# A graph layer on one core: rows of B picked in float32 by partition halves, with counts, copies and node layers rearranged

## The chip, the cores and the metric

The kernel runs on one core of a Trainium2 chip. The time is device microseconds of that core, the median of several runs. A profile is one further execution, recorded by the hardware profiler; its span and its durations are its own.

## What is computed

A message-passing layer on 12,500 nodes with 64 features and 212,500 edges, sorted by `dst`:

```python
h = jnp.maximum(_layernorm(x, axis=-1), 0.0)
edge_in = jnp.concatenate([h[row], h[col], dist], axis=1)      # row = src, col = dst
e = jax.nn.silu(edge_in @ eW1 + eb1)
e = jax.nn.silu(e @ eW2 + eb2)
agg = jax.ops.segment_sum(e, row, num_segments=h.shape[0])
node_in = jnp.concatenate([h, agg], axis=1)
out = x + jax.nn.silu(node_in @ nW1 + nb1) @ nW2 + nb2
```

Everything is float32. The sum goes by `src`, in which the edges are not sorted.

## The kernel before

The first edge product is split: A = h @ eW1[:64] + eb1 and B = h @ eW1[64:128], one row of each for every node, so that an edge needs A[src] + B[dst] + dist * eW1[128]. Both tables lie in HBM (`ta`, `tb`), each row as three bf16 parts that add up to the float32 value.

**Prologue.** `x` is loaded, normalised by five groups of 20 columns, transposed on TensorE, and multiplied to B by `product(1, ...)` (lines 169 to 192), 25 times, four columns each. Edge lists are loaded as 104 rows of 2048; `rowsS` and `auxS` hold, for each edge, its place in a window of B, its bucket, and three bf16 parts of the weight; they go to HBM as `rows` and `aux`.

**Blocks of 1024 edges.** There are 208, in 11 chunks. Since edges are sorted by `dst`, a block needs at most 112 consecutive rows of B, its window `win`. `load` (372) issues on SP the broadcast of the block's places and buckets to 112 partitions (`bc`), the window (384) and the weight's parts (386). `count` (389) runs on VectorE: `pick` (395) is a one-hot matrix of 112 window rows by 1024 edges, `oh` (397) a one-hot of 100 buckets by edges, `run` a running count along the edges (400, a scan that takes its start from `end`, 406), and 408 keeps each edge's own count. `send` (417): TensorE turns the counts into ranks (427) and picks the rows of B plus weight by three bf16 matmuls a tile of 128 edges over 115 rows (435); ScalarE copies them to `qs` (442), VectorE copies the place of the source node beside them (449), and GpSimd scatters 128 rows per indirect DMA to the bucket's free slots in the HBM tensor `q` (454). 1661 such scatters are issued.

**Steps of 512 slots.** 525 steps read `q` back bucket by bucket. `fetch` (489) loads `qt` and `a3` through SP, five batches ahead. Per step, on TensorE: `lr` (521) spreads the places, `pt` transposes the rows (535) and adds the rows of A by a one-hot (542), `p` is the second product (573), `seg` the sum (587). VectorE makes the two one-hots (526, 553) and adds to `aggT` (598); ScalarE computes the two activations (546, 577) and writes the bias (567). `feeds` computes A by `product(0, ...)` beside the first blocks.

**Nodes.** In the last chunk every batch of four node columns ends in `nodes` (333): two `z` products (341 over all 128 partitions, 342 over 64), an activation, and `o` (346 bias, 348 product), then `xr` is added (351).

**Order.** TensorE, VectorE, ScalarE and SP run in the order in which the program is written, by `turn` (605): per step a list of stages of different steps, with four gaps in which a piece of a block, of a feed or of the nodes is put. GpSimd has its own queue. Four PSUM buffers `mm` are shared in turn by `lr`, `pt`, `qp`, `ab`, `z` and `o`. `win` has four fixed buffers, `bc` and `pick` four, `qs` eight.

Of the kernel before, what the change touches and what calls it, by code (L numbers as in the profile page):

```python
# [28 lines left out]
F32 = mybir.dt.float32  # L29
F16 = mybir.dt.float16  # L30
# [10 lines left out]
WL = 112  # L41
BLK = 1024
TB = BLK // P
# [14 lines left out]
def tile_gnn(ctx: ExitStack, tc: tile.TileContext, x, src, dst, ew, eW1, eb1, eW2, eb2, nW1, nb1, nW2, nb2, out):  # L58
# [39 lines left out]
    def rows16(dma, to, of):  # L98

        for part in (slice(0, WL), slice(WL, L)):  # L100
            dma(to[part], of[part])
# [10 lines left out]
    eb1r = const.tile([1, 2, H], F32, name="eb1r")  # L112
    for t in range(2):
        nc.gpsimd.dma_start(eb1r[:, t, :], rows_of(eb1, 1))
# [14 lines left out]
    nb2r = const.tile([1, G, D], F32, name="nb2r")  # L129
    for t in range(G):  # L130
        nc.gpsimd.dma_start(nb2r[:, t, :], rows_of(nb2, 1))
# [14 lines left out]
    nc.vector.tensor_copy(nodes1, nodes_i)  # L146
    ones = const.tile([1, P], F32, name="ones")
# [15 lines left out]
    tb = dram.tile([P * NB, 3 * H], BF16, name="tb")  # L163
    rows = dram.tile([NP, 2, 2, BLK], BF16, name="rows")
    aux = dram.tile([NP, 2, 3, BLK], BF16, name="aux")
# [3 lines left out]
    def product(s, b0, hr, ps, tag, sb, sb2, queue):  # L169

        parts = sb2.tile([P, G, 3, H], BF16, name="parts")
        by = parts.rearrange("l (i a) s h -> l a i s h", a=2)
        rest = sb.tile([P, 2, G // 2, H], F32, name="prest", tag="e1")
        abs_ = []
        for a in range(2):

            half = slice(a * D, (a + 1) * D)
            ab = ps.tile([P, G // 2, H], F32, name="ab", tag=tag)
            if s == 0:
                nc.tensor.matmul(ab, ones, eb1r, start=True, stop=False)  # L180
            for i in range(G // 2):
                nc.tensor.matmul(ab[:, i], hr[half, i, :], w1[half, s, :], start=s == 1, stop=s == 1 or i == G // 2 - 1)
            nc.scalar.copy(by[:, a, :, 0, :], ab)
            abs_.append(ab)
        yield
        for a in range(2):
            nc.vector.tensor_tensor(rest[:, a], abs_[a], by[:, a, :, 0, :], op=OP.subtract)  # L187
        nc.scalar.copy(by[:, :, :, 1, :], rest)
        yield
        nc.vector.tensor_tensor(by[:, :, :, 2, :], rest, by[:, :, :, 1, :], op=OP.subtract)  # L190
        yield
        queue.dma_start(tables[s][:, b0 : b0 + G, :], parts.rearrange("p b s f -> p b (s f)"))
# [4 lines left out]
    base_i = const.tile([1, 2, NP], I32, name="base_i")  # L197
    NW = 4
    wins = [const.tile([P, 3, H], BF16, name=f"win{i}") for i in range(NW)]

    with tc.tile_pool(name="pro", bufs=1) as pro, tc.tile_pool(name="norm", bufs=2) as np_, tc.tile_pool(
# [12 lines left out]
        ewR = pro.tile([NP, PAIR], F32, name="ewR")  # L214
        pad_i = pro.tile([1, PAD], I32, name="pad_i")
        nc.gpsimd.memset(pad_i, N)
        pad_f = pro.tile([1, PAD], F32, name="pad_f", tag="pad_i")
        nc.gpsimd.memset(pad_f, 0.0)
        vec = lambda v, lo, n, m: bass.AP(tensor=v.tensor, offset=v.offset + lo, ap=[[m, n], [1, m]])
        for to, v, pad in (  # L220
            (dstR, dst, vec(dst, E - PAD, 1, PAD)),
            (srcR, src, pad_i),
            (ewR, ew, pad_f),
        ):
            for p0, p1 in ((0, NP // 16 * 16), (NP // 16 * 16, NP - 1)):
                nc.scalar.dma_start(to[p0:p1, :], vec(v, p0 * PAIR, p1 - p0, PAIR))
            nc.scalar.dma_start(to[NP - 1 : NP, :LAST], vec(v, (NP - 1) * PAIR, 1, LAST))
            nc.scalar.dma_start(to[NP - 1 : NP, LAST:], pad)
# [36 lines left out]
        fv = f.rearrange("p (g e) -> p g e", g=2)  # L265
        lo = pro.tile([NP, 2], F32, name="lo")
        nc.vector.tensor_reduce(lo, fv, AX.X, OP.min)
        nc.vector.tensor_scalar(lo, lo, float(N - WL), None, op0=OP.min)
        hi = pro.tile([NP, 2], F32, name="hi")
        nc.vector.tensor_reduce(hi, fv, AX.X, OP.max)  # L270
        lot = nps.tile([1, 2, NP], F32, name="lot", tag="tr")
        for g in range(2):
            nc.tensor.transpose(lot[:, g, :], lo[:, g : g + 1], ident[:NP, :NP])
# [4 lines left out]
        nc.vector.tensor_tensor(  # L278
            rowsS[:, :, 0, :], fv, lo[:, :, None].to_broadcast([NP, 2, BLK]), op=OP.subtract
        )  # L280
# [15 lines left out]
        auxS = pro.tile([NP, 2, 3, BLK], BF16, name="auxS")  # L296
        ev = ewR.rearrange("p (g e) -> p g e", g=2)
        parts3(pro, auxS[:, :, 0, :], auxS[:, :, 1, :], auxS[:, :, 2, :], ev, [NP, 2, BLK], tag="t")
        nc.sync.dma_start(aux, auxS)


# [13 lines left out]

        d3 = pro.tile([P, 3, H], BF16, name="d3")
        parts3(pro, d3[:, 0, :], d3[:, 1, :], d3[:, 2, :], w1d, [P, H])
        for win in wins:
            nc.sync.dma_start(win[WL : WL + 3, :, :], d3[:3, :, :])

# [4 lines left out]
    def nodes_in(B, sb):  # L325
        b = B * G
        xr = sb.tile([L, G, D], F32, name="xr")
        rows16(nc.sync.dma_start, xr, x_rows[:, b : b + G, :])
        hr = sb.tile([P, G // 2, P], F32, name="hrn")
        nc.sync.dma_start(hr, hd[:, b // 2 : b // 2 + G // 2, :])  # L330
        return xr, hr

    def nodes(B, xr, hr, ps, sb, tag):
# [3 lines left out]
        zs = sb.tile([P, 2, G // 2, L], F32, name="zs")  # L337
        for a in range(2):
            half = slice(a * D, (a + 1) * D)
            z = ps.tile([P, G // 2, L], F32, name="z", tag=tag)  # L340
            nc.tensor.matmul(z, w1g, aggT[:, b + a : b + G : 2, :], start=True, stop=False)  # L341
            nc.tensor.matmul(z, w1n[half, :], hr[half, :, :L], start=False, stop=True)  # L342
            nc.scalar.activation(zs[:, a], z, AF.Silu, bias=nb1c)
        yield
        o = ps.tile([L, G, D], F32, name="o", tag=tag)
        nc.tensor.matmul(o, ones[:, :L], nb2r, start=True, stop=False)  # L346
        for t in range(G):
            nc.tensor.matmul(o[:, t, :], zs[:, t % 2, t // 2, :], w2n, start=False, stop=t == G - 1)  # L348
# [8 lines left out]
    with tc.tile_pool(name="ld", bufs=4) as ld, tc.tile_pool(name="ld2", bufs=NQ) as ld2, tc.tile_pool(  # L357
        name="wk", bufs=2
    ) as wk, tc.tile_pool(name="qs", bufs=8) as qsp, tc.tile_pool(name="to", bufs=4) as top, tc.tile_pool(
# [6 lines left out]
        nil = misc[:NB, 2 * TB : 2 * TB + 1]  # L366
        carry = {}
# [4 lines left out]
        def load(s, ahead=0):  # L372

            if s + ahead < nblocks:
                p, g = (s + ahead) // 2, (s + ahead) % 2
                bc = ld.tile([P, 2, BLK], BF16, name="bc")
                r = rows[p, g]
                nc.sync.dma_start(bc[:WL], bass.AP(tensor=r.tensor, offset=r.offset, ap=[[0, WL], [1, 2 * BLK]]))
                blk[s + ahead] = [bc]
            if 0 <= s < nblocks:  # L380
                p, g = s // 2, s % 2
                win = wins[s % NW]
                at = nc.sync.value_load(base_i[:, g, p : p + 1], min_val=0, max_val=N - WL)
                nc.sync.dma_start(win[:WL].rearrange("p s f -> p (s f)"), tb[bass.ds(at, WL), :])
                pick = ld.tile([P, BLK], BF16, name="pick")
                nc.sync.dma_start(pick[WL : WL + 3, :], aux[p, g])
                blk[s] += [win, pick]

        def count(s):
# [4 lines left out]
            bc, win, pick = blk[s]  # L394
            nc.vector.tensor_scalar(pick[:WL, :], bc[:WL, 0, :], part[:WL, :], None, op0=OP.is_equal)
            oh = wk.tile([NB, BLK], F16, name="oh")
            nc.vector.tensor_scalar(oh, bc[:NB, 1, :], part[:NB, :], None, op0=OP.is_equal)
            yield
            run = wk.tile([NB, BLK], F16, name="run")
# [4 lines left out]
            end = wk.tile([NB, 1], F32, name="end")  # L404
            n = min(BLK, E - s * BLK)
            nc.vector.tensor_copy(end, run[:, n - 1 : n])
            carry[c] = end
            nc.vector.tensor_tensor(run, run, oh, op=OP.mult)  # L408
            blk[s].append(run)
# [7 lines left out]
        def send(s):  # L417
# [4 lines left out]
            _, win, pick, run = blk.pop(s)  # L422
# [5 lines left out]
            yield  # L428
            for t0 in range(0, nt, G):
                qs = qsp.tile([P, G, W], F32, name="qs")  # L430
                qp = mm.tile([P, G, H], F32, name="qp", tag="mm")
                m = min(G, nt - t0)
                for t in range(m):
                    for i in range(3):
                        nc.tensor.matmul(  # L435
                            qp[:, t, :],
                            pick[: WL + 3, (t0 + t) * P : (t0 + t + 1) * P],
                            win[: WL + 3, i, :],
                            start=i == 0,
                            stop=i == 2,  # L440
                        )
                nc.scalar.copy(qs[:, :m, :H], qp[:, :m, :])  # L442
# [6 lines left out]
                nc.vector.tensor_copy(  # L449
# [242 lines left out]
    with tc.If(flag > 0):  # L692
        general_sums(tc, N, E, NB, H, src, dst, ew, ta, tb, aggT, w1d, w2, ident, ones, eb2r, part)
# [6 lines left out]
def general_sums(tc, N, E, NB, H, src, dst, ew, ta, tb, aggT, w1d, w2, ident, ones, eb2r, part):  # L700
# [6 lines left out]
    with ExitStack() as ctx:  # L707
# [17 lines left out]
        def tile_of(at, n):  # L725
# [8 lines left out]
            nc.vector.tensor_scalar(pre[:n], w1d[:n], w[:n], None, op0=OP.mult)  # L734
            for k, (idx, table) in enumerate(((si, ta[:]), (di, tb[:]))):
                got = gw.tile([P, 3, H], BF16, name=f"got{k}")
                nc.gpsimd.indirect_dma_start(
                    out=got[:n].rearrange("p s f -> p (s f)"),
# [3 lines left out]
                )  # L742
                v = gw.tile([P, H], F32, name=f"v{k}")
# [79 lines left out]
```

## Time and profile before

| | |
|---|---|
| median of 3 runs | 3326.05 us (3309.03 to 3344.81) |
| profiled execution | 2708.9 us, span 2706.9 us, mean TensorE clock 0.915 |
| TensorE busy | 2321.1 us, 86% of the span |
| weight loads busy | 2168.2 us, 80% |
| VectorE busy | 1846.2 us, 68% |
| GpSimd busy | 1723.0 us, 64% |
| ScalarE busy | 1204.1 us, 44% |
| DMA | 612.85 MB, 226 GB/s over the span |

The profiled execution is 617 us shorter than the median of the runs. Busy times are unions of records: matmuls are pipelined, so the start of one record to the start of the next says what a matmul costs, and its own duration doesn't. One fp32 matmul leaves two records. A line such as L435 is line 435 of the listing above; "PEld" is TensorE's weight load. "Idle before" names what ended the wait of an engine.

### The profile page before, as it was taken

The page shows a single profiled execution, that of the slowest core. Times are in us where ns is not written, and L with a number is a line of the kernel's source. Part 1 is how long each engine was busy: PE and PEld are TensorE (multiplying, and loading weights), DVE is VectorE, ACT ScalarE, POOL GpSimd, SP SyncE. Part 2 cuts the span into 40 slices and gives each one's busy share as a digit, 9 for nine tenths or more (in the row PEclk, how much of TensorE's full clock was granted, in tenths as well). Part 3 has the DMA queues.
Part 4 walks back from the last instruction along what each step waited for, and adds up shares of the span by engine and source line. Part 5 has one row for each costly group of instructions (what it writes and reads, how often), then busy time and mean ns, then how long its engine had stood idle before and what let it go on. Part 6 is the DMA issues. An engine that isn't in the chain of part 4 may idle for free. (4 is left out here: it accounts for less than half of the span.)

```text
span 2706.9 us, 61144 instructions
## 1 busy us (share of the span) xinstructions
PE 2321.1 (86%) x23583; PEld 2168.2 (80%) x23583; DVE 1846.2 (68%) x3287; ACT 1204.1 (44%) x2247; POOL 1723.0 (64%) x1691
## 2 busy tenths in 40 slices
PE   1656688799799699799979979979979979979998
PEld 0445577799699699799879979979979979978886
DVE  5745468688588588678768768868858868743332
ACT  2522234355355355355445435535535545534442
POOL 1036577777777777777777777777777777750000
PEclk9755689899899899999989989989989989989998
DMA  6477867987787697697797787788688758644441
GB/s 180 170 210 208 246 226 227 284 276 231 237 280 244 211 288 247 200 312 245 214 293 254 224 274 252 246 247 269 229 248 272 244 185 267 216 173 127 137 128 33
DMA packets 388692, 612.85 MB, mean 226 GB/s; under 512 B 47232, under 2 KB 294401, under 8 KB 387877
## 3 DMA queue, kind: packets, MB, share of 16 engines
q1 hardware_dynamic: 269560, 423.47, 48.7%
q0 software_dynamic: 53760, 122.94, 13.3%
q10 hardware_dynamic: 65074, 62.46, 9.4%
q8 instruction: 188, 3.08, 0.5%
q14 instruction: 110, 0.90, 0.1%
HBM read 393.49 MB, written 215.18 MB: 225 GB/s over the span
## 5 line engine op out<-in xcount | busy, mean ns | idle before, releaser
L454 POOL DMA_INDIRECT q<-qs,to x1661 | 1710.3, 1030 | 679.2 <-issue 386.4
L546 ACT ACTIVATE e<-pt 128x512 f32<-128x512 f32 x525 | 313.7, 597 | 926.5 <-PE pt L542 765.1
L573 PE MATMUL p<-w,e 128*128 128x128 f32 x4200 | 578.7, 282 | 102.3 <-ACT p L567 102.3
L573 PEld LDWEIGHTS p<-w,e 128*128 128x128 f32 x4200 | 523.6, 196 | 117.1 <-ACT p L567 104.3
L526 DVE TENSOR_SCALAR oneT<-lr,part 125x512 bf16<-125x512 f32 x525 | 392.3, 747 | 325.8 <-PE lr L521 325.7
L587 PE MATMUL seg<-one,e 128*128 128x125 f32 x4200 | 581.2, 282 | 19.8 <-DVE aggT L598 14.6
L587 PEld LDWEIGHTS seg<-one,e 128*128 128x128 f32 x4200 | 523.6, 196 | 22.6 <-ACT qs L442 11.7
L400 DVE TENSOR_TENSOR_SCAN run<-oh,end,misc 100x1024 f16<-100x1024 f16 x197 | 461.1, 2340 | 6.4 <-PE misc L427 5.8
L542 PE MATMUL pt<-oneT,a 125*128 125x256 bf16 (+1 forms) x3300 | 440.1, 272 | 0.0
L435 PE MATMUL qp<-win,pick 115*128 115x128 bf16 x4983 | 369.1, 227 | 37.1 <-DVE oneT L526 30.4
L442 ACT COPY qs<-qp 128x512 f32<-128x512 f32 x416 | 243.3, 585 | 286.5 <-PE qp L435 218.3
L435 PEld LDWEIGHTS <-pick 115*128 115x128 bf16 x4983 | 330.4, 102 | 45.3 <-issue 40.8
L553 DVE TENSOR_TENSOR one<-nodes,qt 128x500 f32<-128x500 f32 x525 | 352.2, 671 | 0.7 <-PE seg L587 0.5
L542 PEld LDWEIGHTS <-a 125*128 125x128 bf16 x3300 | 317.8, 99 | 33.5
L535 PE MATMUL pt<-ident,qt 128*128 128x128 f32 x2100 | 329.5, 281 | 3.1 <-DVE prest L187 2.2
L577 ACT ACTIVATE e<-p 128x512 f32<-128x512 f32 x525 | 313.2, 597 | 12.9 <-PE p L573 9.6
L567 ACT COPY p<-b2f 128x512 f32<-128x512 f32 x525 | 311.8, 594 | 0.0
L598 DVE TENSOR_TENSOR aggT<-aggT,seg 128x500 f32<-128x500 f32 x250 | 168.2, 673 | 152.5 <-PE seg L587 152.3
L521 PE MATMUL lr<-identb,qt 128*125 128x128 bf16 x2100 | 210.6, 224 | 62.2 <-DMA qt<-q 62.2
L521 PEld LDWEIGHTS <-qt 128*125 128x125 bf16 x2100 | 187.2, 140 | 64.0 <-DMA qt<-q 63.3
L535 PEld LDWEIGHTS pt<-ident,qt 128*128 128x128 f32 x2100 | 227.6, 144 | 4.0 <-DVE prest L187 2.3
L408 DVE TENSOR_TENSOR run<-run,oh 100x1024 f16<-100x1024 f16 x208 | 144.3, 694 | 7.1
(118 smaller groups left out, 1264.4 us busy)
## 6 DMA issues: line engine op xcount, KB each, us to landing
qt<-q SPq DMA_DIRECT2D x250, 576.0 KB
a<-ta SPq DMA_DIRECT2D x275, 384.0 KB
bc<-rows SPq DMA_DIRECT2D x208, 448.0 KB
q<-zeros ACTq DMA_DIRECT2D x40, 1462.5 KB
q<-qs,to POOLq DMA_INDIRECT x1661
win<-tb SPq DMA_DIRECT2D x208, 84.0 KB
tb<-parts SPq DMA_DIRECT2D x25, 384.0 KB
ta<-parts SPq DMA_DIRECT2D x25, 384.0 KB
```

The source lines that it names most:

```text
L400: nc.vector.tensor_tensor_scan(run, oh, nil.to_broadcast([NB, BLK]), carry.get(c, 0.0), op0=OP.add, op1=OP.add)
L435: nc.tensor.matmul(qp[:, t, :], pick[: WL + 3, (t0 + t) * P : (t0 + t + 1) * P], win[: WL + 3, i, :], start=i == 0, stop=i == 2,)
L454: i = nc.gpsimd.indirect_dma_start(out=q[:], out_offset=bass.IndirectOffsetOnAxis(ap=to[:k, t : t + 1], axis=0), in_=qs[:k, t - t0, :], in ...
L521: nc.tensor.matmul(lr[:L, t, :], loc[:, at : at + 1].to_broadcast([P, L]), identb, start=True, stop=True)
L526: nc.vector.tensor_scalar(oneT, st[k].pop("lr")[:L], part1[:L, :], None, op0=OP.is_equal)
L535: nc.tensor.matmul(pt[:, t, :], qt[:, j, :H], ident, is_transpose=True, start=t == 0, stop=False, skip_group_check=True)
L542: nc.tensor.matmul(pt[:, cols, :], a3[:L, b, i, :], oneT[:, cols, :], start=False, stop=i == 2, skip_group_check=True)
L546: nc.scalar.activation(e1, pt, AF.Silu)
L553: nc.vector.tensor_tensor(one, nodes1[:, None, :].to_broadcast([P, G, L]), qt[:, j : j + G, H : H + 1].to_broadcast([P, G, L]), op=OP.is_e ...
L573: nc.tensor.matmul(p2[:, t, :], e1[:, t, :], w2, start=False, stop=t == G - 1, skip_group_check=True)
L577: nc.scalar.activation(e2, p2, AF.Silu)
L587: nc.tensor.matmul(item[2][:, b, :], e2[:, t, :], one[:, t, :], start=j % n == 0, stop=j % n == n - 1)
```

## The change

Windows of B become two per block, each of at most 48 rows for 512 edges, one in partitions 0 to 47 and one in 64 to 111; partitions 48 and 49 of each half hold the weight's row of eW1 and the bias eb1, and the matching rows of `pick` the edge's weight and 1. `tb`, `win` and `pick` are float32, so one fp32 matmul over 50 partitions takes the place of three bf16 ones; all eight of a block are issued before the copies, alternating between the halves. The weight is loaded from the input itself into `pick`, after the one-hot is written. The bias matmul leaves `product(0)`; nb2 is added to `xr` on GpSimd. `run` is float32, its last column is the next scan's start, and the product goes to a new f16 tile. The copy of the places moves to ScalarE. In `nodes` both `aggT` products come first, then both halves' products. `rows` loads are split into a half-block and a block load. The path for inputs that don't fit (`general_sums`) is adapted.

```diff
-WL = 112
+WL = 48
+HB = 64
+HALF = BLK // 2
...
+    same = const.tile([P, 1], F32, name="same")
+    plus = const.tile([P, 1], F32, name="plus")
+    nc.vector.tensor_scalar(plus, part, HB - 0.5, None, op0=OP.is_gt)
+    nc.vector.scalar_tensor_tensor(same, plus, -float(HB), part, op0=OP.mult, op1=OP.add)
+    nc.vector.tensor_scalar(plus, same, float(WL + 1), None, op0=OP.is_equal)
+    nc.vector.scalar_tensor_tensor(same, plus, -1e6, same, op0=OP.mult, op1=OP.add)
...
-    tb = dram.tile([P * NB, 3 * H], BF16, name="tb")
+    tb = dram.tile([P * NB, H], F32, name="tb")
-    aux = dram.tile([NP, 2, 3, BLK], BF16, name="aux")
...
+        if s:
+            got = sb2.tile([P, G, H], F32, name="got")
+            for a in range(2):
+                nc.scalar.copy(got.rearrange("l (i a) h -> l a i h", a=2)[:, a], abs_[a])
+            yield
+            queue.dma_start(tables[s][:, b0 : b0 + G, :], got)
+            return
...
-            if s == 0:
-                nc.tensor.matmul(ab, ones, eb1r, start=True, stop=False)
...
+    wins = [const.tile([P, H], F32, name=f"win{i}") for i in range(NW)]
+    for win in wins:
+        nc.vector.memset(win, 0.0)
+        for a in range(2):
+            for i, row in enumerate((w1d, eb1b)):
+                at = a * HB + WL + i
+                nc.gpsimd.dma_start(win[at : at + 1, :], row[:1, :])
...
-        parts3(pro, auxS[:, :, 0, :], auxS[:, :, 1, :], auxS[:, :, 2, :], ev, [NP, 2, BLK], tag="t")
-        nc.sync.dma_start(aux, auxS)
...
+        nc.gpsimd.tensor_tensor(xr, xr, nb2b[:L, None, :].to_broadcast([L, G, D]), op=OP.add)
...
+        z = [ps.tile([P, G // 2, L], F32, name="z", tag=tag) for _ in range(2)]
+        for a in range(2):
+            nc.tensor.matmul(z[a], w1g, aggT[:, b + a : b + G : 2, :], start=True, stop=False)
         for a in range(2):
             half = slice(a * D, (a + 1) * D)
-            z = ps.tile([P, G // 2, L], F32, name="z", tag=tag)
-            nc.tensor.matmul(z, w1g, aggT[:, b + a : b + G : 2, :], start=True, stop=False)
-            nc.tensor.matmul(z, w1n[half, :], hr[half, :, :L], start=False, stop=True)
-            nc.scalar.activation(zs[:, a], z, AF.Silu, bias=nb1c)
+            nc.tensor.matmul(z[a], w1n[half, :], hr[half, :, :L], start=False, stop=True)
+        for a in range(2):
+            nc.scalar.activation(zs[:, a], z[a], AF.Silu, bias=nb1c)
...
-        nc.tensor.matmul(o, ones[:, :L], nb2r, start=True, stop=False)
...
-                bc = ld.tile([P, 2, BLK], BF16, name="bc")
-                nc.sync.dma_start(bc[:WL], bass.AP(tensor=r.tensor, offset=r.offset, ap=[[0, WL], [1, 2 * BLK]]))
+                bc = ld.tile([P, HALF], BF16, name="bc")
+                of = bass.AP(tensor=r.tensor, offset=r.offset, ap=[[HALF, 2], [0, HB], [1, HALF]])
+                nc.sync.dma_start(bc, of)
+                bb = ld.tile([P, BLK], BF16, name="bb")
+                nc.sync.dma_start(bb[:112], bass.AP(tensor=r.tensor, offset=r.offset + BLK, ap=[[0, 112], [1, BLK]]))
...
-                nc.sync.dma_start(pick[WL : WL + 3, :], aux[p, g])
+                for a in range(2):
+                    h = 2 * g + a
+                    at = nc.sync.value_load(base_i[:, h, p : p + 1], min_val=0, max_val=N - WL)
+                    nc.sync.dma_start(win[a * HB : a * HB + WL, :], tb[bass.ds(at, WL), :])
+                pick = ld.tile([P, HALF], F32, name="pick")
+        def weights(s):
...
+                    of = bass.AP(tensor=ew.tensor, offset=ew.offset + e0, ap=[[HALF, 2], [1, HALF]])
+                    nc.sync.dma_start(pick[WL::HB, :], of)
...
-            nc.vector.tensor_scalar(pick[:WL, :], bc[:WL, 0, :], part[:WL, :], None, op0=OP.is_equal)
+            nc.vector.tensor_scalar(pick, bc, same, plus, op0=OP.is_equal, op1=OP.add)
...
+            weights(s)
             nc.vector.tensor_tensor_scan(
                 run, oh, nil.to_broadcast([NB, BLK]), carry.get(c, 0.0), op0=OP.add, op1=OP.add
             )
             yield
-            nc.vector.tensor_copy(end, run[:, n - 1 : n])
+            end = run[:, n - 1 : n]
             carry[c] = end
-            nc.vector.tensor_tensor(run, run, oh, op=OP.mult)
+            own = wk.tile([NB, BLK], F16, name="own")
+            nc.vector.tensor_tensor(own, run, oh, op=OP.mult)
...
+            qps = [mm.tile([P, G, H], F32, name="qp", tag="mm") for _ in range(2)]
+            for t in range(G):
+                for a in range(2):
+                    half = slice(a * HB, a * HB + WL + 2)
+                    if a * G + t < nt:
+                        nc.tensor.matmul(
+                            qps[a][:, t, :], pick[half, t * P : (t + 1) * P], win[half, :], start=True, stop=True
+                        )
...
-                nc.vector.tensor_copy(
+                nc.scalar.copy(
                     qs[:, :m, H:], locE[:, at : at + m, p][:, :, None].to_broadcast([P, m, W - H])
                 )
```

## The prediction

> **What bounds the kernel now.** I read the table of windows first, with edges where GpSimd's work begins and ends, because the page's average (PE 86%, POOL 64%) mixes stages. Its columns are window, length, then busy time and count of PE, weight loads, DVE, ACT and POOL, clock, DMA share, GB/s.
>
> ```profile
> 60.00:147.00 87.00, 53.18 (x265) 39.50 (x264) 63.12 (x113) 48.93 (x114) 0.00 (x0) 0.70 0.46 167
> 147.00:172.00 25.00, 10.96 (x46) 6.54 (x47) 10.22 (x18) 3.26 (x7) 0.00 (x0) 0.50 0.73 196
> 172.00:420.00 248.00, 182.99 (x1386) 148.34 (x1384) 138.37 (x265) 71.22 (x144) 170.00 (x164) 0.67 0.75 228
> 420.00:2417.00 1997.00, 1799.38 (x19873) 1749.30 (x19870) 1509.52 (x2700) 958.97 (x1767) 1539.18 (x1496) 0.95 0.78 246
> 2417.00:2707.00 290.00, 270.10 (x2001) 221.50 (x2001) 95.18 (x156) 107.71 (x204) 1.16 (x2) 0.95 0.38 120
> ```
>
> The fourth row is the kernel: 1496 indirect DMAs in 1997 us, one per 1.335 us. GpSimd looks 77% busy, but its timeline shows no room:
>
> ```profile
> 1410.73 0.97 POOL L454 DMA_INDIRECT q<-qs,to  x1 [0.30 <-issue]
> 1412.00 1.17 POOL L454 DMA_INDIRECT q<-qs,to  x1 [0.30 <-DMA q<-qs,to]
> 1413.48 0.97 POOL L454 DMA_INDIRECT q<-qs,to  x1 [0.30 <-issue]
> ```
>
> A scatter starts every 1.27 us, 0.97 busy and a fixed 0.30 of issue; some are stretched. So the middle advances at eight scatters a block, 8 x 1.335 = 10.7 us, whatever TensorE does. TensorE is close behind. From its timeline
>
> ```profile
> 1303.10 0.64 PE L535 MATMUL pt<-ident,qt 128*128 128x128 f32 x4
> 1303.57 0.82 PE L542 MATMUL pt<-oneT,a 125*128 125x256 bf16 x6
> 1304.23 1.06 PE L573 MATMUL p<-w,e 128*128 128x128 f32 x8
> 1305.12 1.05 PE L587 MATMUL seg<-one,e 128*128 128x125 f32 x8
> 1306.02 0.83 PE L435 MATMUL qp<-win,pick 115*128 115x128 bf16 x12
> 1306.69 0.39 PE L521 MATMUL lr<-identb,qt 128*125 128x128 bf16 x4
> ```
>
> I take differences of starts, since printed times overlap: a step costs 0.23 (lr) + 0.47 + 0.66 + 0.89 + 0.90 = 3.15 us, and twelve qp matmuls 0.67. About 475 of 525 steps run beside 187 blocks: 2.54 steps, 8.0 us, plus 1.34 for qp and 0.2 for ranks: 9.5 us at full clock, 10.0 at the granted 0.95, of 10.7. Last, the tail after 2417 us: the chain of waits there is nearly all TensorE, one batch of four node columns per 10.39 us.
>
> ```profile
> 2505.81 0.59 PE L341 MATMUL z<-aggT,w1g 128*128 128x250 f32 x2
> 2506.33 0.69 PE L342 MATMUL z<-hrn,w1n 64*128 64x250 f32 x2
> 2506.95 0.69 PE L341 MATMUL z<-aggT,w1g 128*128 128x250 f32 x2
> 2507.57 0.69 PE L342 MATMUL z<-hrn,w1n 64*128 64x250 f32 x2
> 2508.18 1.16 PE L573 MATMUL p<-w,e 128*128 128x128 f32 x8
> 2509.27 0.69 PE L346 MATMUL o<-nb2r,ones 1*125 1x256 f32 x2
> 2509.89 1.08 PE L348 MATMUL o<-w2n,zs 128*125 128x64 f32 x8
> ```
>
> [...] L341 to L342 is 128 rows to 64: a z record pair takes about 0.42 us of streaming (two 250-column records 0.21 apart), but the pairs start 0.62 apart, so a change of mode costs about 0.2 us. And in the prologue the two halves' fp32 products ran at once:
>
> ```profile
> 61.55 1.23 PE L182 MATMUL ab<-w,hT 64*128 64x128 f32 x8
> 63.98 1.22 PE L182 MATMUL ab<-w,hT 64*128 64x128 f32 x4 [1.20 <-DVE prest L187]
> ```
>
> Eight records (both halves) took 1.23 us, four (one half) 1.22. [...] between 500 and 2300 us, 84% of the scatters that ran beside L397 took over 1.11 us, 59% of those beside L408 and 43% of those beside L553, but 9% of those beside the scan L400. [...] L408, all f16, took 694 ns for 1024; L290, f32, 2283 for 2048.
>
> **The change, part by part.**
>
> Rows of B. Out: 24 bf16 qp records a block, 24 x 55 ns (0.67/12) = 1.34 us. In: eight fp32 matmuls on 50 rows, two records each, 111 ns a record as in L573 (0.89/8). Were the halves one after the other: 16 x 0.111 = 1.78 us. Running at once: 0.89. Two mode changes add 0.4. So 1.29 (gain 0.05 a block) or 2.18 us (loss 0.84). I take the first because of the 1.23/1.22 pair, though that was on a cold clock with four records per half in a row and not alternating; both ends stay. Middle: nothing, covered by GpSimd's 10.7 us.
>
> Two qp buffers are now taken at once from the four of mm, so lr and the next pt wait one allocation sooner for DVE's oneT behind a 2.34 us scan. Today qp waited for oneT seven times, 30 us in all. Taken at nothing; cover: TensorE's 0.7 us a block.
>
> VectorE. Out per block: pick 483, end 148, two place copies 404 ns. In: pick on 512 elements, bf16 to f32, nearest row L285 (2048 f32 in 1221 ns), so about 360 (bounds 300 and 750, the latter L526 from PSUM); the product of f32 and f16 loses the 16-bit rate: 1024 x 1.115 = 1.14 us against 0.69. Scan unchanged (2.34), a wider output being its only risk. Net about -0.2 us a block; not on the path. What it can do is stretch scatters: they average 1.335 against 1.27, some 0.065 x 1661 = 105 us in all. More two-input time (91 us over the run), less pick: I take 0, bounds -20 and +30.
>
> ScalarE gains two place copies a block: L442 took 265 ns for 128 elements and 586 for 512, so 64 cost about 0.21; 0.42 x 208 = 87 us in an engine 48% busy in the middle. Scatters wait for it, but up to eight qs buffers stand between.
>
> Loads. SP issues bc, bb, two win and the weights, five for three (about 0.35 us each) and two register loads for one, some 1.2 us a block more; SP spends 819 us of the run waiting for L553 to free qt, so it has time. New wait: the weights' load waits for pick on VectorE, with qt, a and bc behind it in SP's queue; qp is three pieces, one block, later. SP's rows for the old aux load are 0.36 us of issue; I assume 5 to 10 us to land under a busy DMA, inside 10.7. A late one stalls qp and everything behind it on TensorE. Bytes a block fall from 448+84+6 to 128+224+48+4 KB, 28 MB of 613 in all: covered.
>
> Prologue (60 to 147 us). Each of 25 B products loses two L187 (0.42), one L190 (0.69) and one L188 (ACT, 0.62): 38 us of VectorE's 63, and DMA per batch 256 KB for 384; splitting the weights loses two L158/L160 (4.6). What is late next: ScalarE (49 less 19), the norm's reductions and TensorE's cold transposes. I take -25 us, bounds -10 and -40. GpSimd gets 16 small loads at 0.5 us each at the start, idle then.
>
> Feeds (172 to 420): 100 bias records L180 (574 ns) and their mode changes go. GpSimd ran at 248/164 = 1.51 us a scatter here, so 164 x 0.18 = 29 us were lost to others; I take -10, bounds 0 and -25.
>
> Tail. z: four 128-row records 0.85, one change 0.2, halves at once 0.42, a change 0.2: 1.67 for 2.37 (2505.81 to 2508.18). o: eight records of weights-bound 0.109 are 0.87 us, for 1.64 now (2510.82, where seg starts, less 2509.18, where eight p records of 0.111 and a mode change after 2508.18 end). Together about -1.5 us of 10.39, over 24 batches -36; bounds -28 and -45; if halves ran in turn, -26. GpSimd's 25 adds of nb2 fall after its last scatter at 2417 and five batches ahead of use: nothing at up to 1 us each.
>
> Sum: -25 - 10 - 36 = -71 of the profiled execution's 2708.9 us, 2.6%. The median of the runs is 3326, 23% above it, and no view says why. Taken as a share that gives 3239, taken as microseconds 3255; I say **3240**, the share, since the stages that shrink would be longer too.
>
> **The rivals.**
> - A, the forecast, GpSimd keeps the middle: bounds of the sum -38 to -130 (prologue, feeds, tail and scatters together), so 3165 to 3285. Chance 0.50.
> - B, the halves run one after another[...]: TensorE becomes the bound. 8.0 + 0.2 + 2.18 = 10.4 us a block, 10.9 at clock 0.95; it decides above 10.7, and with the waits TensorE has today (about 10% of the window) it stands at about 11.6: +0.9 x 187 = +170, less 65: +105, about 3430. For: an fp32 weight load lasts 192 ns (L587), a qp load 98. Against: the 1.23/1.22 pair. Chance 0.20.
> - C, covered by something else: the prologue is held by its transfers, scatters stretch by 0.02 us (+33) and late weights take the tail's gain: 3300 to 3350. Chance 0.14.
> - D, the runs are 23% longer because TensorE is slower in them than in the profile. Then its own work counts everywhere: tail 36, bias records and their changes 45, prologue 25, times up to 1.4, is 106 to 150: 3220 to 3176, and with the 0.05 us of qp and fewer stalls on loads perhaps 3100. Against: nothing shown measures it. Chance 0.16.
> - That the change doesn't do what it says: the built order shows 1661 qp matmuls for 4983 and no bias matmuls, so no.
>
> **The numbers.** Faster than 1% is A and D, slower is B, within 1% C (1% is about what a measurement of this kernel can tell). The range 3130 to 3400 takes A, C, most of D and B's lower part.
>
> **What would show it.** Right: 1.33 us a scatter in the middle, first scatter near 145 us, tail period near 8.8 us, qp pairs starting together and the block's qp about 1.3 us. Wrong: qp near 2.2 us and scatters spaced by TensorE; qp waiting for the weights' DMA; scatters above 1.36 us.

## The result, and where the profile after shows it

The changed kernel takes 3417.85 us (3414.80 to 3440.46, four runs), the kernel before 3331.55 (3309.03 to 3344.81): ratio **1.0281, interval 1.0208 to 1.0354, slower**. The forecast was 3240.

One thing must be known to read any number here. Whole sets of runs (kernels timed together on one chip) stand at one of two levels, for every kernel in the set: the kernel before took about 2710 us in some, 3330 to 3420 in the others. The profile that the prediction was made from is of the first level (span 2706.9), the comparison above of the second. I call them the short and the long level, and compare only within one.

At the short level a twin of the changed kernel (below, t1) stood at 1.0023 [1.0014, 1.0032]: no gain, no loss. Its windows, and then those of the changed kernel at the long level, with edges at the first and last scatter and near the 165th (columns as in the prediction):

```profile
139.00:392.00 253.00, 126.16 (x1186) 113.58 (x1188) 148.90 (x216) 78.11 (x194) 178.44 (x165) 0.65 0.72 218
392.00:2466.00 2074.00, 1778.49 (x18303) 1681.51 (x18299) 1552.76 (x2129) 994.14 (x2130) 1590.18 (x1496) 0.93 0.70 224
2466.00:2714.00 248.00, 227.38 (x1951) 205.15 (x1951) 95.61 (x156) 103.19 (x204) 19.11 (x26) 0.96 0.44 140
```

```profile
144.00:420.00 276.00, 135.75 (x1088) 119.20 (x1088) 139.99 (x203) 73.37 (x181) 172.72 (x163) 0.61 0.64 189
420.00:3155.00 2735.00, 2218.95 (x18212) 1964.95 (x18211) 1563.47 (x2127) 986.72 (x2122) 1626.95 (x1498) 0.85 0.54 171
3155.00:3415.00 260.00, 245.58 (x2142) 223.24 (x2141) 105.43 (x172) 114.41 (x225) 19.98 (x26) 0.98 0.44 134
```

The second rows hold nearly the same number of scatters, 1496 and 1498 (1496 in the prediction's row from 420 to 2417): they took 1997 us before, 2074 in the short twin, 2735 at the long level, where TensorE's clock is 0.85. The first scatter comes earlier (139 and 144 us for 172) and the tail is shorter (248 for 290). Stage by stage, in us, from the scatters' starts (e1 is the changed kernel again, in a set where before took 3418; e2 a twin of before, in one where it took 3406):

```
                    first scatter   first to last   after last   span
short  before          172.1           2245.5         289       2706.9
short  t1 (changed)    139.1           2327.0         248       2714.1
long   e2 (before)     182.8           2937.8         300       3420.5
long   e1 (changed)    144.5           3099.8         262       3505.9
```

So prologue and tail gain 74 us (short) and 76 (long), somewhat more than forecast (61), and the stretch between gives back 82 and 162. The long pair comes from two sets and e2 starts its scatters late (two other variants of the kernel before, p1 and f2 below, start at 173 and 171). A pair whose kernels before stand within 1 us says nearly the same: from first to last the changed kernel's first profile took 3011.1 us, p1, which leaves that stretch as it was, 2857.9: 153 more. The tail's batches in the changed kernel:

```profile
3200.41 1.01 PE L348 MATMUL z<-aggT,w1g 128*128 128x250 f32 x4
3201.35 0.69 PE L351 MATMUL z<-hrn,w1n 64*128 64x250 f32 x4
3201.97 1.16 PE L604 MATMUL p<-w,e 128*128 128x128 f32 x8
3202.97 0.98 PE L357 MATMUL o<-w2n,zs 128*125 128x64 f32 x8
3203.78 1.11 PE L618 MATMUL seg<-one,e 128*128 128x125 f32 x8
```

z is now 1.56 us from start to start (2.37 before), o 0.81 (1.64); the period of a batch went from 10.39 to 8.77 us. In the kernel before, o's records (called weights-bound in the prediction) start 0.109 us apart at 64 columns, as their weight loads do, and p's 0.112 at 128.

What the middle loses differs by level. **Short:** GpSimd still paces it: between 420 and 2400 us 99.7% of the gaps between two scatters are the fixed 0.30 us (0.35 at most) in the kernel before, 98.5% in t1. Its scatters are stretched by the new VectorE product. GpSimd's timeline and VectorE's, in t1:

```profile
1405.97 0.96 POOL L486 DMA_INDIRECT q<-qs,to  x1 [0.30 <-issue]
1407.24 1.81 POOL L486 DMA_INDIRECT q<-qs,to  x1 [0.31 <-DVE one L585]
1409.37 1.07 POOL L486 DMA_INDIRECT q<-qs,to  x1 [0.30 <-issue]
```

```profile
1407.00 1.22 DVE L438 TENSOR_TENSOR own<-run,oh 100x1024 f16<-100x1024 f32 x1
```

The scatter that starts beside the float32 x float16 product lasts 1.81 us for 0.97. Over the run a scatter that touches that product takes 0.47 us more than the undisturbed 0.965 on average (0.18 beside the all-float16 product before); the mean of all went from 1030 to 1065 ns. 35.6 ns x 1661 = 59 us of the 82. The rest is idle time between scatters, 536 us before and 558 in t1; nine gaps of 1.0 to 3.2 us, one at a chunk border each, are together 15 us longer than the fixed 0.30. At eight of these borders TensorE stands still for 19 to 25 us ahead of `qp`. The profile names the weights' load for four of these waits and nothing for the other four ("issue", 91.3 us in all; waits of TensorE in t1, with total, times and longest):

```profile
PE qp L465 <- DMA pick<-in_edge_weight_dram: 103.5, 11, 25.5
...
PE pt L567 <- DVE oneT L558: 62.6, 31, 10.2
```

Not all of it is new: the kernel before stops at the same borders, for 13 to 16 us ahead of `p` and 3 to 6 ahead of `qp`, and there GpSimd doesn't fall idle.

**Long:** the scatters are no longer 1.27 us apart in a row; 12 to 13% of the gaps are longer than 0.35 us, in the kernel before (e2) as in the changed one. GpSimd's timeline in the changed kernel:

```profile
1409.43 0.96 POOL L485 DMA_INDIRECT q<-qs,to  x1 [0.30 <-issue]
1416.02 1.81 POOL L485 DMA_INDIRECT q<-qs,to  x1 [5.62 <-ACT p L598]
1418.14 0.96 POOL L485 DMA_INDIRECT q<-qs,to  x1 [0.30 <-issue]
```

It idles 5.62 us because its next rows come late. TensorE, which makes them, stops in the middle of its products, waiting for nothing that the profile shows:

```profile
1103.29 1.05 PE L464 MATMUL qp<-win,pick 50*128 50x128 f32 x8
1104.80 0.47 PE L464 MATMUL qp<-win,pick 50*128 50x128 f32 x2 [0.45 <-issue]
1105.52 0.27 PE L464 MATMUL qp<-win,pick 50*128 50x128 f32 x1 [0.25 <-issue]
1106.23 0.38 PE L464 MATMUL qp<-win,pick 50*128 50x128 f32 x2 [0.44 <-issue]
```

After eight records the others come one or two per 0.71 us. In the waits of TensorE these stops lead the list, in the kernel before too (e2: 143.2 us ahead of qp); what is new in the changed kernel is its fourth line:

```profile
PE qp L464 <- issue: 165.5, 271, 3.8
PE p L604 <- issue: 64.0, 102, 1.5
PE seg L618 <- issue: 60.6, 99, 1.2
PE pt L566 <- DVE oneT L557: 58.7, 31, 6.7
```

### The profile page after: what moved, and what is told of

Read it like the earlier page. It is cut to its first block, busy times and chain, and to the rows that moved or that the text cites. A ratio compares the mean times of both kernels' runs of the same rounds, so it can differ in the third digit from the quotient of the medians.

```text
span 3415.2 us, 59029 instructions
## 1 busy us (share of the span) xinstructions
PE 2658.2 (78%) x21774; PEld 2351.4 (69%) x21774; DVE 1875.3 (55%) x2593; ACT 1221.9 (36%) x2634; POOL 1837.8 (54%) x1727
## 5 line engine op out<-in xcount | busy, mean ns | idle before, releaser
L485 POOL DMA_INDIRECT q<-qs,to x1661 | 1800.7, 1084 | 1324.0 <-ACT qs L480 612.6
L604 PE MATMUL p<-w,e 128*128 128x128 f32 x4200 | 694.9, 312 | 85.0 <-issue 64.0
L618 PE MATMUL seg<-one,e 128*128 128x125 f32 x4200 | 665.3, 303 | 76.4 <-issue 60.6
L604 PEld LDWEIGHTS p<-w,e 128*128 128x128 f32 x4200 | 617.2, 223 | 142.7 <-issue 97.7
L618 PEld LDWEIGHTS seg<-one,e 128*128 128x128 f32 x4200 | 599.7, 217 | 95.7 <-issue 86.5
L573 PE MATMUL pt<-oneT,a 125*128 125x256 bf16 (+1 forms) x3300 | 512.8, 297 | 41.1 <-issue 40.3
L464 PE MATMUL qp<-win,pick 50*128 50x128 f32 x3322 | 372.9, 321 | 184.1 <-issue 165.5
L429 DVE TENSOR_TENSOR_SCAN run<-oh,run,misc 100x1024 f32<-100x1024 f16 x197 | 461.0, 2340 | 97.6 <-remote 72.5
L464 PEld LDWEIGHTS qp<-win,pick 50*128 50x128 f32 x3322 | 283.3, 213 | 259.8 <-issue 230.1
L437 DVE TENSOR_TENSOR own<-run,oh 100x1024 f16<-100x1024 f32 x208 | 253.5, 1219 | 0.1
```

Source lines behind the costliest of these rows:

```text
L429: nc.vector.tensor_tensor_scan(run, oh, nil.to_broadcast([NB, BLK]), carry.get(c, 0.0), op0=OP.add, op1=OP.add)
L464: nc.tensor.matmul(qps[a][:, t, :], pick[half, t * P : (t + 1) * P], win[half, :], start=True, stop=True)
L485: i = nc.gpsimd.indirect_dma_start(out=q[:], out_offset=bass.IndirectOffsetOnAxis(ap=to[:k, t : t + 1], axis=0), in_=qs[:k, t - t0, :], in ...
L573: nc.tensor.matmul(pt[:, cols, :], a3[:L, b, i, :], oneT[:, cols, :], start=False, stop=i == 2, skip_group_check=True)
L604: nc.tensor.matmul(p2[:, t, :], e1[:, t, :], w2, start=False, stop=t == G - 1, skip_group_check=True)
L618: nc.tensor.matmul(item[2][:, b, :], e2[:, t, :], one[:, t, :], start=j % n == 0, stop=j % n == n - 1)
```

## The experiments

**The levels (e0, e1, e2).** The kernel before alone; the changed kernel again; and a twin of the kernel before:

```diff
     nc.gpsimd.memset(zeros, 0.0)
+    nc.gpsimd.memset(zeros, 0.0)
```

> The kernel before, unchanged, so that a profile of it in the regime of the timed runs can be read. Theory 1 (TensorE's own queue is the bound in the timed runs of both kernels, which the first profile of the kernel before did not show): span 3300 to 3350 us, scatters 1.6 to 1.75 us apart, and hundreds of gaps of 0.5 to 2 us between TensorE records that wait for nothing. Theory 2 (the timed runs are longer for a cause outside TensorE, such as slower transfers): same span, scatters still 1.33 us apart or waiting for DMA, no such gaps. Theory 3 (the first profile was an ordinary execution and time is lost outside the profile): a span near 2707 us.

> The changed kernel, unchanged, beside the kernel before in the same call: before was 3332 us where it was timed and 2709 us in its profile and when run again, so the comparison is made once more where both can be read. Theory 1 (the changed kernel itself makes TensorE starve for instructions): about 3400 us wherever it runs, with before at 2708, a ratio near 1.26. Theory 2 (two conditions of the chip, in one of which TensorE stops for instructions in both kernels; in the other the sum of the prediction holds): near 2640 us where before is 2708, scatters about 1.34 us apart. Theory 3 (middle): 2720 to 2800 us, no starving, but scatters stretched by the longer VectorE product (own, 1219 ns) to 1.38 or more.

> The kernel before with one memset of the zeros tile issued twice, so another program with the same work. Before alone took 2708 us, beside the changed kernel 3332 and 3418. Theory 1 (the longer time comes with a second, different program in the call, or with the chip that was given; TensorE then stops for instructions in either kernel): both near 3330 to 3420 us, with hundreds of stops of 0.5 to 2 us on TensorE in the twin's profile, scatters about 1.7 us apart. Theory 2 (only the changed kernel brings it about): both near 2708 us.

Measured: e0 2709.14; e1 3507.06 beside 3417.82, ratio 1.0258 [1.0228, 1.0288]; e2 3422.42 beside 3406.38. I took the long level for the effect of a second program in the set. It is not: two later sets with four and three programs beside the kernel before stood at the short level. One chip showed both levels. The cause stays open.

**One part undone, or alone (u1, u2, u3, p1; long level).** u1 puts the counts back to float16 (L425 to L438 of the changed kernel), and with them the second buffer of `oh` and `run` that the change had dropped; u2 the place copies back to VectorE, u3 both; p1 is the kernel before with the new node layers (L343 to L362 of the changed kernel) and nb2 added on GpSimd, alone.

```diff
-                nc.scalar.copy(
+                nc.vector.tensor_copy(
                     qs[:, :m, H:], locE[:, at : at + m, p][:, :, None].to_broadcast([P, m, W - H])
```

> The changed kernel with the counts back in f16 (run, end, product in place: VectorE 694 + 148 ns for 1219 a block). The changed kernel stands at 1.026 to 1.028 of before. Theory V (VectorE's longer product delays oneT and stretches scatters, and so slows the middle): 0.995 to 1.012, scatter duration back to about 1040 ns from 1089. Theory Q (the fp32 picking itself, with its mode changes and two PSUM buffers at once): unchanged, 1.02 to 1.03. Theory S (ScalarE's place copies): unchanged.

> The changed kernel with the place copies back on VectorE (202 ns each there, 256 on ScalarE). Theory S (ScalarE is late with e1 and the bias because of them): 1.00 to 1.015. Theory V: worse than the changed kernel, 1.03 to 1.05, since VectorE has 0.4 us a block more. Theory Q: unchanged, 1.02 to 1.03.

> Both undone: what is left is the picking, the loads, the prologue and the nodes. The prologue and the nodes take some 28 + 36 us off, 0.981 of before, if nothing else counts. Theory Q: the picking costs the middle the rest, 1.02 to 1.03 still. Theories V and S: 0.98 to 1.00.

> The kernel before with the node layers rearranged alone (both z first, then both halves; no bias matmul; nb2 added on GpSimd). All theories: the tail's period falls from 10.39 to 8.77 us as it did in the changed kernel, 24 x 1.62 = 39 us, so 0.985 to 0.991 of before; the middle unchanged.

Measured: u1 1.0382 [1.0336, 1.0427], u2 1.0141 [1.0075, 1.0207], u3 1.0182 [1.0127, 1.0238], **p1 0.9885 [0.9813, 0.9957]**. The node layers are a gain, of 38 us where 39 were expected, and the only version that beats both kernels at this level. The place copies cost something: with them on VectorE the time falls by 1.2 to 1.4% (changed kernel, in its two comparisons, to u2) and 1.9% (u1 to u3). The counts are not the loss at this level: with float16 the mean scatter falls from 1083 (e1) to 1039 ns, so the float32 product does stretch the scatters, yet u1 is slower than the changed kernel. GpSimd doesn't pace here.

**What paces the middle (f1, g1; short level).** More TensorE work, and more GpSimd work:

```diff
-            for t in range(nt):
-                nc.tensor.matmul(rank[:, t : t + 1], ...
+            for _ in range(3):
+                for t in range(nt):
+                    nc.tensor.matmul(rank[:, t : t + 1], ...
```

> The kernel before with the eight rank matmuls of every block issued three times (the same result written again): 16 more matmuls a block on TensorE, start to start 25 ns in the traces, so 0.40 us a block and 83 us over 208 blocks; nothing is added elsewhere. If GpSimd's scatters set the middle in these runs, as the prediction took from the first profile: within 10 us of the kernel before, ratio 1.00. If TensorE sets it: 80 to 110 us longer, ratio 1.024 to 1.033, and the scatters further apart than the 1.78 us of the twin. If a denser TensorE is granted the full clock more often, and that is worth more than the matmuls cost: faster than the kernel before, with less than 25% of the stretch from 500 to 2400 us at half clock.

> The kernel before with a memset of 128x256 on GpSimd ahead of the scatters of each half block: about 0.28 us each (577 ns is measured for 128x576), 0.55 us a block, 115 us over 208 blocks; TensorE is given nothing more. If GpSimd sets the middle: about 115 us longer, ratio 1.03 to 1.04. If TensorE sets it: under 30 us, ratio 1.00 to 1.01.

Measured: f1 1.0044 [1.0027, 1.0061], 14 us for 83 us of TensorE: most of it is covered, so TensorE doesn't pace here; with the scatters back to back as above, GpSimd does. g1 1.003 [1.0022, 1.0039] tells nothing: its memsets depend on nothing, and the trace has all 416 of them before 182 us. They never ran in the middle.

**The same at the long level (f2).** The ranks five times:

> The kernel before with the rank matmuls issued five times: 32 more matmuls a block, 0.80 us of TensorE, 166 us over 208 blocks. Where the kernel before takes about 2709 us, three times (83 us) gave 14 us. If GpSimd sets the middle there, about 0.7 us a block of it are covered: 20 to 80 us, 1.01 to 1.03. Where it takes about 3330 us: if TensorE sets the middle in that condition, 160 to 230 us, 1.048 to 1.07; if the stops are waits for something else (GpSimd, transfers), under 60 us, below 1.02.

Measured: **1.1645 [1.1563, 1.1728], 552 us** for 166 us of products, well above the 160 to 230 expected of a TensorE that sets the pace. TensorE's timeline, first of f1 (short), then of f2 (long):

```profile
1306.77 0.74 PE L428 MATMUL misc<-ones,run 100*128 100x1 f16 x24
```

```profile
1407.32 0.49 PE L428 MATMUL misc<-ones,run 100*128 100x1 f16 x14
1408.01 0.24 PE L428 MATMUL misc<-ones,run 100*128 100x1 f16 x4 [0.20 <-issue]
1408.74 0.24 PE L428 MATMUL misc<-ones,run 100*128 100x1 f16 x4 [0.49 <-issue]
1409.46 0.28 PE L428 MATMUL misc<-ones,run 100*128 100x1 f16 x5 [0.48 <-issue]
1410.88 0.21 PE L428 MATMUL misc<-ones,run 100*128 100x1 f16 x2 [1.14 <-issue]
```

24 in a row at 25 ns in f1; in f2 fourteen at that pace, then four or five per 0.72 us. From first to last the ranks of a block take 0.58 us in f1 and on average 3.85 in f2, where 40 x 25 ns would be 1.0; in e2, with eight, they take 0.22. The added 3.63 us x 208 are 755 us, and 552 of them show in the kernel's time. So at the long level TensorE sets the time, and bursts of short products are one place where it stops. What holds its instructions back no view shows.

**Two buffers at once (r1, r2, b2; short level).** r1 is the changed kernel, r2 is u2, each with one half picked in each piece and one mm buffer at a time. b2 is the kernel before with its own bf16 products, all 24 in one piece into two buffers:

```diff
-            for t0 in range(0, nt, G):
-                qp = mm.tile([P, G, H], F32, name="qp", tag="mm")
+            qps = [mm.tile([P, G, H], F32, name="qp", tag="mm") for _ in range(2)]
...
-                if todo and len(doing) < 3:
+                if todo and len(doing) < 1:
```

> The changed kernel with one half of a block picked in each of its two pieces again, one mm buffer at a time; the float32 products stay, but the two halves of the partitions no longer work beside each other. In the instruction order the lr products that wait for VectorE fall from 186 to 9, as in the kernel before. If the two buffers taken at once make the loss: the 45 to 60 us of waits for oneT are gone, and the ratio falls from 1.026 to 1.028 to 1.015 or less, in spite of up to 0.9 us more of TensorE a block. If TensorE's own time in the picking decides: 0.9 us x 208 = 185 us more at most, ratio 1.04 to 1.08. If neither decides (stops and clock): 1.02 to 1.035.

> The changed kernel with the place copies on VectorE (1.014 alone where the kernel before takes about 3330 us) and one half picked in each piece, one mm buffer at a time (lr products waiting for VectorE 8 for 186). If the two buffers at once are the rest of the loss there: the waits of pt for oneT are gone and it comes to 0.985 to 1.000. If TensorE's own time for the halves one after another decides: 1.03 to 1.08. If neither: 1.007 to 1.02. Where the kernel before takes about 2709 us the split alone stood at 1.023, and 1.015 to 1.03 is expected.

> The kernel before with its own bf16 picking, but all 24 products of a block in one piece, into two mm buffers taken at once, as the changed kernel does (and the table products of one batch at a time in flight, not three, since the buffers do not allow more). In the instruction order lr products that wait for VectorE rise from 9 to 185. If the two buffers at once cost the change its loss where the kernel before takes about 3330 us: 45 to 65 us of waits of pt for oneT appear, and it is slower by 1.5 to 3%. If the loss is in the new operations and loads: within 0.8%. Where the kernel before takes about 2709 us GpSimd covers it: within 0.8% in both.

Measured: r1 1.023 [1.0213, 1.0247], r2 1.0238 [1.0208, 1.0269], b2 1.0327 [1.0303, 1.0351]. r1's waits of TensorE:

```profile
PE pt L560 <- DVE oneT L551: 4.6, 8, 1.7
```

The waits for oneT went from 62.6 us (t1) to 4.6, so they do come from the two buffers. (The kernel before has waits for oneT too, 30.4 us, but ahead of `qp`.) Yet r1 is 58 us slower than t1: halves one after the other are dearer than the waits. Each half now takes TensorE 1.085 us, 2.17 a block, where both together take 1.09 in t1. The scatters stand 1.419 us apart on average (1.386 in t1), but 97% of the gaps are still the fixed 0.30 us: the loss lies at the chunk borders, where GpSimd now idles up to 6.9 us and, soon after, up to 3.9. In b2 the waits appear (43 us), but most of its 90 us are not theirs. Its window beside that of the kernel before shows where they are:

```profile
172.00:420.00 248.00, 128.59 (x807) 99.64 (x805) 90.34 (x178) 45.95 (x90) 112.31 (x112) 0.56 0.59 167
```

112 scatters where there were 164, and 85 us later at the 165th: the table products, one batch in flight for three, hold up the start (from 172 to 520 us TensorE waits 122 us for the loads of `hr` that they need, 39 in the kernel before). That second edit spoils the total. After 500 us b2 runs at 10.77 us a block for 10.67, so the two buffers cost about 0.1 us a block at the short level, 20 us. At the long level it wasn't tried.

**Control (t1; short level).** The changed kernel with the memset twice.

> The changed kernel with the memset of zeros in the prologue issued twice, under 1 us: a control for how far a program that does the same work can move. If what runs beside the change is of no weight: 1.023 to 1.031, as the changed kernel's two comparisons. If the place of the program or its timing decides TensorE's stops: outside that, anywhere from 1.01 to 1.04.

Measured: 1.0023 [1.0014, 1.0032]. It was meant as a control at the long level; it is the changed kernel's only measurement at the short one.

**The weights' queue (w1, w2, w3; long level).** The load of the weights (L411 of the changed kernel) from ScalarE's queue; w2 with float16 counts too, w3 with the place copies on VectorE as well:

```diff
-                    nc.sync.dma_start(pick[WL::HB, :], of)
+                    nc.scalar.dma_start(pick[WL::HB, :], of)
```

> The changed kernel with the weights' load (L410 to L416) issued by ScalarE's queue and not SP's; nothing else. Where the kernel before takes about 2709 us: the twin of the changed kernel stood at 1.0023 there, with TensorE waiting 101 us in ten waits of up to 25 us at the chunk borders for the weights' row of pick, and nine gaps of 3 us in the scatters. If SP's queue (the weights behind a qt load that waits for the last scatters of a chunk) causes these: the waits for pick are gone, the gaps too, 20 to 40 us less, ratio 0.988 to 0.995. If the weights wait for their data or for VectorE: 1.000 to 1.005. Where the kernel before takes about 3330 us the waits for pick are under 10 us in all, and nothing is to be had: 1.020 to 1.033.

> The same, and the counts in f16 again as in the kernel before. Where the kernel before takes about 2709 us: if the float32 product L437 (1.2 us, two inputs) stretches the scatters beside it, the mean scatter goes from 1064 ns to about 1030, 35 ns x 1661 = 58 us less: 0.966 to 0.978. If the scatters are stretched by something else of the change (copies on ScalarE, loads): within 10 us of the run with the weights alone. Where it takes about 3330 us: counts alone gave 1.038 for 1.026, so 1.02 to 1.04.

> The same, and the place copies on VectorE again: left of the change are the picking, its loads and base tables, and the node layers. Where the kernel before takes about 2709 us: prologue 30, tail 40 and feeds 10 of the prediction's sum and a middle as before: 0.966 to 0.978; if it is slower than the run before by over 0.5%, the place copies are better on ScalarE. Where it takes about 3330 us: 1.010 to 1.025, as without the weights' move (1.018).

Measured: 1.0492 [1.0414, 1.0569], 1.0529 [1.0434, 1.0625], 1.0234 [1.0154, 1.0315]. A miss: w1 is worse by 2% than with the load on SP (1.0258, 1.0281, in other sets), for a reason that isn't shown, and the short level, where its waits cost, wasn't met. It gives a third pair for the place copies: 2.8% from w2 to w3.

**Packets (b1; short level).** The kernel before with the bc load in two.

> The kernel before with the load of bc in two, 112 rows of 2 KB twice where it was 112 rows of 4 KB: the same bytes, 112 packets and one issue of SP's more a block (the change has about 128 packets and five loads for three). If smaller packets and more issues cost the change its loss: slower by 1% or more where the kernel before takes about 3330 us. If not: within 0.6%.

Measured: 1.0017 [1.0003, 1.0031]. More and smaller packets cost 0.3% at most at the short level, where GpSimd covers much; at the long level they weren't tried.

## Why the prediction was wrong

Right, by its own steps:
- Prologue, -25: first scatter at 139 to 147 us for 172, -25 to -33.
- Tail, -36: -38 to -41, period 8.77 us where 8.8 was named; GpSimd's adds of nb2, put at up to 1 us each, took 0.73 (L336 of the changed kernel, median).
- The halves run at once: 16 records in an undisturbed burst start within 0.89 us, and the picking takes 1.09 us a block (1.29 named). The "cold clock" of the pair that this rests on shows as pace alone: no clock record stands before 91.5 us, but four records of the transposes beside it (L252) took 1.11 to 1.49 us, the same form at 2512 us (L535) 0.61. r1 is rival B as a kernel: 2.17 us of picking (B said 2.18) and 11.35 us a block (B said 11.6), though at the short level GpSimd stays the pacer between the chunk borders.
- GpSimd paces the middle at the short level, with TensorE close behind (f1).

**The step that failed is "Middle: nothing, covered by GpSimd's 10.7 us"**, resting on "the middle advances at eight scatters a block, 8 x 1.335 = 10.7 us, whatever TensorE does".
- That bound was read off a profile of 2709 us, where the runs took 23% longer. The prediction said so ("no view says why") and scaled the sum by 1.23 all the same. In the runs TensorE paces (f2), at 14.2 us a block (e2) to 15.1 (e1), so the cover of 0.7 us is gone and a wait put on TensorE can count. Rival D named a slower TensorE, but let it enlarge the gains only; it didn't ask what becomes of the edits that were costed at nothing.
- "Two qp buffers ... taken at nothing": 43 to 66 us of waits of pt for oneT in all eight long profiles with the new picking, at most 0.4 in those without it, which wait up to 8 us for oneT ahead of qp. That they are as much of the 162 us is argued from the trace; no experiment undid the two buffers at the long level.
- Place copies on ScalarE, "up to eight qs buffers stand between": 1.2 to 2.8% in three pairs at the long level (the first of them across sets). Why is not settled.
- "Scatters ... I take 0, bounds -20 and +30": +59 us at the short level, twice the bound. L438 took 1.22 us with one of its inputs in float32 (1.14 forecast; 0.69 before, all in float16), the pick 0.54 (0.36), but the size that counted was the scatter's stretch beside the product, 0.47 us where 0.18 was seen.
- Weights' load: the named sign, qp waiting for it, came at the short level, mostly at the chunk borders: 103.5 us of TensorE's time (part of it in place of the waits there before), and some 15 us of idle time of GpSimd. "5 to 10 us to land" became waits of up to 25. At the long level qp waits 5 us for it at most. That qt's load ahead of it on SP is the reason wasn't shown.
- Feeds, -10: 253 us for 248 to the 165th scatter (252 in e0, the kernel before again); nothing gained.
- A slip in a sum: A's bounds, "-38 to -130", leave out the +30 of the scatters that they name. With it they are -8 to -130, 3165 to about 3316; 3418 lies outside either way.

Short level: -33, -41 and +82 make +8 of 2707, and 7 were measured; stretched scatters (59) and idle time between them (22) account for the 82 in the traces. No run at this level undid one of the two. Long level: 43 to 66 us of oneT waits and 40 to 95 for the places would leave 0 to 80 of the 162 us open, if they add up, which isn't shown. From first to last scatter TensorE's idle time grew by 119 us from e2 to e1 (571 to 690): 39 of waits for oneT, 21 of stops, 59 of everything else; its busy time grew by 43, with 261 us more at half clock. Programs differ at this level by 1% for no reason that I found (u1 against the changed kernel), so I don't settle it.

## What to carry to other kernels

If the median of the runs is far above the profiled span, the profile may show another bound than the runs have: cost every edit twice, once under each engine that could pace, before calling it covered. An edit that is hidden behind the pacing engine is only as free as that engine is surely the pacer; added waits on the next engine are a debt. And of two good parts (node layers: 0.9885 alone) measure each alone, since the rest of a change can bury them.

## What the runs showed that I had not expected

- The two levels, 2709 and 3330 to 3420 us, for the same program.
- TensorE's clock records hold only the values 1.0 and 0.5, and the shortest half-clock stretches are 3.41 us. At the short level, between 500 and 2400 us, the 3.41 us ahead of such a stretch are nearly idle (TensorE busy 4% at the median in the kernel before, 0 in t1), and hardly a product lies in the half-clock time (444 of 19139 before). At the long level that isn't so: e1 has 109 such stretches there, but no idle time of TensorE over 3.0 us; in the 3.41 us ahead of them its records cover 44% at the median and up to 69%. There the clock falls to half although work goes on:

```
500 to 2400 us     at half clock   us a block there   at full clock
before (short)        172 us            10.2              10.7
e2 before (long)      481               21.3              12.8
changed (long)        559               20.7              13.1
e1 changed (long)     621               22.7              13.0
p1 nodes (long)       437               19.3              12.7
```

  Longer times tend to go with more half-clock time, but not strictly: e2 took 3422 us with 481, the changed kernel 3417 with 559. Whether it is cause or mark wasn't tried.
- The stops have a beat: between 500 and 2400 us of e2, 41% follow the one before after 0.65 to 0.80 us, 31% after about 1.43, and none sooner than 0.65. A late arrival of instructions would be a rival cause, but the trace doesn't show it. The 16 KB transfers of the queue marked "instruction" (188 in e2, 240 in f2, 52 more for the 13312 weight loads and products that f2 adds, so I take them to bring TensorE's) take as long at both levels, 1.06 us at the median before and 1.03 in e2, and the stops stand evenly in the time from one transfer to the next.
- A scatter beside a two-input VectorE product with a float32 operand was 0.47 us longer on average at the short level; beside the same product in float16 0.18.
